# Ordering every engine by hand in a fused GNN and mixture-of-experts attention kernel, with a one-copy way out of PSUM for o

## The chip, the cores and the metric

The kernel runs on one core of a Trainium2 chip. The metric is the device time of one launch in microseconds; of several runs the median is given. Engines: TensorE (PE, its weight loads PEld), VectorE (DVE), ScalarE (ACT), GpSimd (POOL) and SyncE (SP). SP and POOL issue the DMAs that are spoken of here.

## The reference

A graph layer over 1250 nodes is followed by a block of attention with mixtures of experts and a feed-forward net. Only the second half of the attention is touched. With 16 heads of 64, 8 experts, 2 chosen, and rows of 1024:

```
q, k = rope(x Wq), rope(x Wk)                     # 16 heads of 1250 x 64
gv, go = gate(x, Wsel_v), gate(x, Wsel_o)         # sigmoid, top 2 of 8
v   = einsum('bsd,bhse,hedp->bhsp', x, gv, Wv)    # all 8 experts, gated sum
att = softmax(q k^T / sqrt(64))
o   = einsum('bhst,bhtp->bhsp', att, v)
y   = einsum('bhsp,bhse,hepd->bsd', o, go, Wo)    # added to the normalised input
```

Everything is float32. The kernel splits each factor of a product into a rounded part `hi` and the rest `lo`, and forms three matmuls, hi·hi, hi·lo, lo·hi (`dot`, lines 141 to 145). ACT rounds (`w_hi`, `att_hi`, `go_hi`), DVE subtracts (`w_lo`, `att_lo`, `go_lo`).

## The kernel before

Three Python generators issue the work, and the one that is not leading is stepped once per piece of the leading one.

- `values` leads first. Per head it splits four weight tiles of 128 x 1024 (`weights`, lines 123 to 134: load on SP into one of two `w_raw` buffers, `w_hi` on ACT, `w_lo` on DVE; five pairs of buffers are in rotation), then makes ten blocks of v. A block is 24 matmuls of 512 columns in four pieces of six. DVE multiplies a block by its gates (`ve`, line 808), and after every second block adds the experts in a tree (lines 814 to 819).
- `attention` runs under it, in chunks of 256 queries, five to a head and eighty in all, each of eight pieces. A chunk has two softmax blocks: PE makes `side`, DVE the maximum `most` (line 710), ACT the exp `p` (line 711). `turn` then moves the two blocks by 16 DMAs into `turned` (line 724), half issued by SP and half by POOL, DVE transposes within 32 x 32 blocks (line 787), and `split` makes `att_hi` and `att_lo` in five parts (lines 737, 738). `product` multiplies each part with v into the one PSUM tile `po` (line 751). v holds hi in columns 0 to 63 and lo in 64 to 127, so `po` has two halves of 64 rows, which belong together. Chunk n's softmax, chunk n-1's first two products and chunk n-2's last three lie in the same eight pieces.
- `outputs` leads after `values`, and the last pieces of `attention` run under it. Per pair of heads and half of the experts it splits four tiles of Wo, and in five steps of 250 nodes loads o (`oc`), 1/sum (`r`) and the gates (`gb`), multiplies them (lines 841, 850), splits the result (lines 853, 855), makes four groups of twelve matmuls, and adds each to `acc` (line 870). Then `feed_forward` follows.

The end of a product group is this; `po` has a single buffer, and the next group waits until both lines have read it:

```
nc.scalar.copy(o, po[HD:])                        # line 757, ACT
nc.vector.tensor_tensor(o, po[:HD], o, ALU.add)   # line 758, DVE
```

The order of PE is that of the program text in `values`, in `attention` and in the outputs that run with it (a manual schedule for PE alone). The order of the other engines there, and of all in the rest, is chosen by the framework's scheduler.

Of the kernel before, what the change touches and what calls it, by code (L numbers as in the profile page):

```python
# [22 lines left out]
N = 1250  # L23
# [49 lines left out]
def gnn_ffn_kernel(  # L73
# [31 lines left out]
    o_d = [dram.tile([P, N], F32, name=f"o_d{j}") for j in range(NP)]  # L105
# [11 lines left out]
    gate_v = base.tile([P, NT, P], F32, name="gate_v")  # L117
# [5 lines left out]
    def weights(block, lo_engine=None, raw=None):  # L123

        if raw is None:
            raw = raws[0].tile([P, D], F32, name="w_raw")
        nc.sync.dma_start(raw, block)
        pool = ring.pop(0)
        ring.append(pool)
        hi = pool.tile([P, D], F32R, name="w_hi")  # L130
        nc.scalar.copy(hi, raw)  # L131
        lo = pool.tile([P, D], F32R, name="w_lo")
        (lo_engine or nc.vector).tensor_tensor(lo, raw, hi.bitcast(F32), ALU.subtract)  # L133
        return hi, lo
# [54 lines left out]
    with ExitStack() as gctx:  # L189
# [314 lines left out]
        z_ctx = ctx.enter_context(ExitStack())  # L504
        zpool = z_ctx.enter_context(tc.tile_pool(name="zpool", bufs=1, side="right"))
# [16 lines left out]
    zpool2 = z_ctx.enter_context(tc.tile_pool(name="zpool2", bufs=1, side="right"))  # L522
# [156 lines left out]
    def attention(pool):  # L679
# [11 lines left out]
        def load(n):  # L691

            h, c = chunks[n]
            if c == 0:
                nc.gpsimd.dma_start(keys[:, :N], kq_d[h][:, 0, :].bitcast(F32R))
            q_of[n] = pool.tile([P, 2, QW], F32R, name="q", bufs=2)
            c0 = min(QW * c, N - QW)
            nc.gpsimd.dma_start(q_of[n], kq_d[h][:, 1:, c0 : c0 + QW].bitcast(F32R))

        def softmax(n, i):  # L700
# [12 lines left out]
            if i == 1:  # L713
                del q_of[n]

        def turn(n):
# [4 lines left out]
            for b in range(NA):  # L721
                for a in range(NA):
                    queue = nc.gpsimd if (a + b) % 2 else nc.sync
# [9 lines left out]
        def split(n, k):  # L733

            x = turned[n].rearrange("p t (A k) -> p (t A) k", A=NA)[:, :, 2 * NB * k : 2 * NB * (k + 1)]
            hi, lo = (pool.tile([P, 2 * NA, 2 * NB], F32R, name=name, bufs=3) for name in ("att_hi", "att_lo"))
            nc.scalar.copy(hi, x)  # L737
            nc.vector.tensor_tensor(lo, x, hi.bitcast(F32), ALU.subtract)  # L738
            parts_of[n, k] = hi, lo

        def product(n, k):
            h, c = chunks[n]
            if k == 0:
                sum_of[n] = psums[-1].tile([P, QW], F32, name="po", bufs=1)
            po = sum_of[n]
            parts = parts_of.pop((n, k))
            for b in range(2):
                t = 2 * k + b
                rows = min(P, N - P * t)
                for part in parts:  # L750
                    nc.tensor.matmul(po, lhsT=v_of[h][:rows, t, :], rhs=part[:rows, :, NB * b : NB * (b + 1)],  # L751
                                     start=(t == 0 and part is parts[0]), stop=(t == NT - 1 and part is parts[1]))
            if t < NT - 1:
                return
            del sum_of[n], turned[n]
            o = pool.tile([HD, QW], F32, name="o", bufs=1)
            nc.scalar.copy(o, po[HD:])
            nc.vector.tensor_tensor(o, po[:HD], o, ALU.add)  # L758
            j, h2 = divmod(h, 2)
            c0, new = min(QW * c, N - QW), QW * c  # L760
            to = o_d[j][HD * h2 : HD * (h2 + 1), c0 : c0 + QW]
            if (2 * n) % 3 < 2:
                nc.sync.dma_start(to[:, new - c0 :], o[:, new - c0 :])
            else:

                nc.sync.dma_start(to[:, new - c0 : P], o[:, P + new - c0 :])
                nc.sync.dma_start(to[:, P:], o[:, :P])

        load(0)
        for n in range(len(chunks) + 2):  # L770
            now, last, before = (0 <= m < len(chunks) for m in (n, n - 1, n - 2))
            for piece in range(8):
                if now and piece in (0, 3):
                    softmax(n, piece // 3)
                if piece == 3 and n + 1 < len(chunks):
                    load(n + 1)
                if now and piece == 3:
                    turn(n)
                if now and piece == 5 and chunks[n][1] == NC - 1:
                    sums(chunks[n][0])  # L780
                if before and piece in (1, 2, 4):
                    product(n - 2, min(piece + 1, 4))
                if last and piece > 5:
                    product(n - 1, piece - 6)
                if last and piece == 2:
                    for i in range(2):
                        nc.vector.transpose(turned[n - 1][:, i], turned[n - 1][:, i])  # L787
                if last and piece > 2:
                    split(n - 1, piece - 3)
                yield  # L790


    def values(att_pool, pool):
        for h in range(H):
            w = [weights(wv[h, k]) for k in range(4)]
            v_of[h] = att_pool.tile([P, NT, P], F32R, name="v2", bufs=2)
            for t in range(NT):
                n = min(P, N - P * t)
                p = bank([n, 512])
                for d in range(ND):  # L800
                    dot(p, z_of(t, d), [part[:, 512 * (d % 2) : 512 * (d % 2 + 1)] for part in w[d // 2]],
                        d == 0, d == ND - 1)
                    if d % 2 and d < ND - 1:
                        yield
                gate = gate_v[:n, t, NX * h : NX * (h + 1)]
                if t % 2 == 0:
                    ve = pool.tile([P, 2, NX, HD], F32, name="ve", bufs=1)
                nc.vector.tensor_tensor(ve[:n, t % 2], p.rearrange("p (e k) -> p e k", e=NX),
                                        gate[:, :, None].to_broadcast([n, NX, HD]), ALU.mult)
                if t % 2:  # L810
                    for n, k in ((P, slice(0, 2)),) if n == P else ((P, slice(0, 1)), (n, slice(1, 2))):
                        x = ve[:n, k]
                        for half in (4, 2):
                            nc.vector.tensor_tensor(x[:, :, :half], x[:, :, :half], x[:, :, half : 2 * half], ALU.add)
                        v = pool.tile([P, 2, HD], F32, name="v")[:n, k]
                        nc.vector.tensor_tensor(v, x[:, :, 0], x[:, :, 1], ALU.add)
                        v2 = v_of[h][:n, t - 1 + k.start : t - 1 + k.stop, :]
                        nc.vector.tensor_copy(v2[:, :, :HD], v)
                        nc.vector.tensor_tensor(v2[:, :, HD:], v, v2[:, :, :HD].bitcast(F32), ALU.subtract)
                yield  # L820
# [4 lines left out]
    def outputs(acc_pool, pool):  # L825
        last = QW * (NC - 1)
        for j in range(NP):
            for half_e in range(2):
                first = j == 0 and half_e == 0
                w = [weights(wo[j, 4 * half_e + i]) for i in range(4)]  # L830
                for c in range(NQ):
                    o = pool.tile([P, QB], F32, name="oc", bufs=1)
                    nc.sync.dma_start(o, o_d[j][:, QB * c : QB * (c + 1)])
                    r = pool.tile([P, QB], F32, name="r", bufs=1)
                    for h2 in range(2):
                        for a, b in ((QB * c, min(QB * (c + 1), last)), (max(QB * c, last), QB * (c + 1))):
                            if b > a:
                                at_ = a + (NC * QW - N if a >= last else 0)
                                nc.sync.dma_start(r[HD * h2 : HD * (h2 + 1), a - QB * c : b - QB * c],
                                                  r_d[j][h2 : h2 + 1, at_ : at_ + b - a].to_broadcast([HD, b - a]))  # L840
                    nc.vector.tensor_tensor(o, o, r, ALU.mult)
# [189 lines left out]
```

## Time and profile before

| what | value |
|---|---|
| median of three runs | 3069.24 us (3068.29 to 3071.58) |
| profiled execution | 3064.65 us, its span 3062.8 us |
| mean granted TensorE clock | 0.975 |
| busy share of PE, DVE, ACT, POOL | 94%, 69%, 33%, 16% |
| values and attention, from the first `turned` to the last product | 637.8 to 2056 us |
| first output matmul | 1953.3 us |
| output matmuls end | 2935.9 us |

A line of a group reads: source line, engine, operation, out<-in with the tiles' names, shape, count | busy time in us, mean ns of one | idle time of the engine just before, and what ended most of it. Matmuls are pipelined and overlap, so that the distance from start to start tells their rate. A wait for several things is put down to the one that came last.

### The profile page before, as it was taken

Reading aid. Unit: us, or ns where it says so; the run is one execution under the profiler, and the core shown is the slowest. Engines: PE = TensorE matmul, PEld = TensorE weight load, DVE = VectorE, ACT = ScalarE, POOL = GpSimd, SP = SyncE. Lnnn points to the kernel's source line nnn. Section 1 sums busy time; section 2 is a strip of 40 time slices with the busy share of each in tenths; the row PEclk is TensorE's granted clock in tenths of the full one; section 3 lists DMA queues with packets and bytes.
Section 4 is the critical chain, followed back from the end, with each engine's and each line's share of the span. In section 5 each row is a group of like instructions: output and inputs, shape, how many; then the busy total and the mean of one; then the engine's idle time right before and its main releaser. Section 6 shows DMA issues by size and latency. Waiting matters only on the chain. (4 is left out here: it accounts for less than half of the span.)

```text
span 3062.8 us, 40809 instructions
## 1 busy us (share of the span) xinstructions
PE 2883.5 (94%) x14018; PEld 2367.9 (77%) x14018; DVE 2099.1 (69%) x3731; ACT 1015.6 (33%) x1706; POOL 504.7 (16%) x838
## 2 busy tenths in 40 slices
PE   6989899999999999999998999789999999999998
PEld 5777799877777888777777887567777777777787
DVE  7975588567777787777776777665555555555685
ACT  5762223234444344434443344321111112111222
POOL 2000011123233232322322232110000000000023
PEclk9999899999999999999999999889999999999999
DMA  3115455635555555555554556755334334334312
GB/s 114 54 42 184 142 160 160 199 94 141 126 128 123 128 130 136 133 125 126 140 126 108 128 129 158 167 131 146 97 98 116 97 91 117 97 98 119 91 41 94
DMA packets 241546, 370.10 MB, mean 121 GB/s; under 512 B 61929, under 2 KB 191273, under 8 KB 241170
## 3 DMA queue, kind: packets, MB, share of 16 engines
q1 hardware_dynamic: 191854, 263.25, 31.7%
q0 software_dynamic: 47616, 93.93, 13.4%
q10 hardware_dynamic: 1860, 10.24, 1.1%
q8 instruction: 111, 1.82, 0.2%
q14 instruction: 105, 0.86, 0.1%
HBM read 210.49 MB, written 57.04 MB: 87 GB/s over the span
## 5 line engine op out<-in xcount | busy, mean ns | idle before, releaser
L145 PE MATMUL mm<-w_hi,go_lo 128*125 128x512 f32 x1280 | 507.7, 401 | 21.9 <-DVE go_lo L855 21.5
L143 PE MATMUL mm<-w_hi,go_hi 128*125 128x512 f32 x1280 | 510.6, 399 | 12.1 <-ACT go_hi L853 11.3
L143 PE MATMUL mm<-w_hi,zT 128*128 128x512 f32 (+1 forms) x1280 | 512.2, 400 | 0.0
L144 PE MATMUL mm<-w_lo,go_hi 128*125 128x512 f32 x1280 | 512.1, 400 | 0.0
L145 PE MATMUL mm<-w_hi,zT 128*128 128x512 f32 (+1 forms) x1280 | 511.7, 400 | 0.0
L144 PE MATMUL mm<-w_lo,zT 128*128 128x512 f32 (+1 forms) x1280 | 511.1, 399 | 0.0
L724 POOL DMA_DIRECT2D turned<-p x640 | 341.3, 542 | 355.3 <-ACT p L711 250.1
L737 ACT CAST att_hi<-turned 128x512 fp32r<-128x512 f32 x400 | 237.2, 619 | 440.3 <-PE po L751 187.7
L145 PEld LDWEIGHTS mm<-w_hi,go_lo 128*125 128x125 f32 x1280 | 240.9, 188 | 94.6 <-DVE go_lo L855 34.3
L710 DVE TENSOR_REDUCE most<-side 128x1 f32<-128x1250 f32 x160 | 232.6, 1454 | 116.2 <-PE side L707 104.7
L711 ACT ACTIVATE p<-side,most 128x1250 f32<-128x1250 f32 x160 | 209.0, 1306 | 309.9 <-DVE most L710 308.5
L738 DVE TENSOR_TENSOR att_lo<-turned,att_hi 128x512 fp32r<-128x512 f32 x400 | 262.8, 686 | 55.8 <-ACT att_hi L737 54.9
L143 PEld LDWEIGHTS mm<-w_hi,go_hi 128*125 128x125 f32 x1280 | 240.7, 188 | 72.8 <-ACT go_hi L853 12.2
L787 DVE STREAM_TRANSPOSE turned<-turned 128x1280 f32<-128x1280 f32 x160 | 232.3, 1490 | 92.6 <-DMA o_d<-o 63.3
L751 PE MATMUL po<-att_hi,v 128*128 128x256 f32 (+1 forms) x800 | 219.4, 295 | 78.6 <-DVE o L758 75.2
L145 PEld LDWEIGHTS mm<-w_hi,zT 128*128 128x128 f32 (+1 forms) x1280 | 241.3, 189 | 61.8
L853 ACT CAST go_hi<-gb 128x500 fp32r<-128x500 f32 x160 | 98.2, 614 | 571.6 <-PE mm L144 540.4
L144 PEld LDWEIGHTS mm<-w_lo,go_hi 128*125 128x125 f32 x1280 | 240.1, 188 | 58.8
L850 DVE TENSOR_TENSOR gb<-gb,oc 128x500 f32<-128x500 f32 x160 | 101.6, 676 | 251.2 <-DMA gb<-g_d 250.6
L144 PEld LDWEIGHTS mm<-w_lo,zT 128*128 128x128 f32 (+1 forms) x1280 | 241.9, 189 | 36.1
L143 PEld LDWEIGHTS mm<-w_hi,zT 128*128 128x128 f32 (+1 forms) x1280 | 241.7, 189 | 36.1
L133 DVE TENSOR_TENSOR w_lo<-w_raw,w_hi 128x1024 fp32r<-128x1024 f32 x154 | 187.6, 1218 | 103.1 <-ACT w_hi L131 102.9
(207 smaller groups left out, 4642.2 us busy)
## 6 DMA issues: line engine op xcount, KB each, us to landing
turned<-p SPq DMA_DIRECT2D x640, 80.0 KB
turned<-p POOLq DMA_DIRECT2D x640, 80.0 KB, 3.6
gb<-g_d SPq DMA_DIRECT2D x160, 250.0 KB
w_raw<-in_wv SPq DMA_DIRECT2D x64, 512.0 KB
w_raw<-in_wo SPq DMA_DIRECT2D x64, 512.0 KB
q<-kq_d POOLq DMA_DIRECT2D x80, 256.0 KB, 3.2
kq_d<-qk_hi SPq DMA_DIRECT2D x64, 156.2 KB
kq_d<-qk_lo SPq DMA_DIRECT2D x64, 156.2 KB
```

The lines of the kernel that those rows point to most:

```text
L133: (lo_engine or nc.vector).tensor_tensor(lo, raw, hi.bitcast(F32), ALU.subtract)
L143: nc.tensor.matmul(p, lhsT=lhs[0], rhs=rhs[0], start=start, stop=False)
L144: nc.tensor.matmul(p, lhsT=lhs[0], rhs=rhs[1], start=False, stop=False)
L145: nc.tensor.matmul(p, lhsT=lhs[1], rhs=rhs[0], start=False, stop=stop)
L710: nc.vector.tensor_reduce(most, side[:, :N], AX.X, ALU.max, negate=True)
L711: nc.scalar.activation(p[:, (2 * n + i) % 3, :N], side[:, :N], AF.Exp, bias=most, accum_out=inverse[h][:, 2 * c + i : 2 * c + i + 1])
L724: queue.dma_start(t[NB * a : NB * (a + 1), :, KA * b : KA * (b + 1)], both[NB * b : NB * (b + 1), :, KA * a : KA * (a + 1)])
L737: nc.scalar.copy(hi, x)
L738: nc.vector.tensor_tensor(lo, x, hi.bitcast(F32), ALU.subtract)
L751: nc.tensor.matmul(po, lhsT=v_of[h][:rows, t, :], rhs=part[:rows, :, NB * b : NB * (b + 1)], start=(t == 0 and part is parts[0]), stop=(t ...
L787: nc.vector.transpose(turned[n - 1][:, i], turned[n - 1][:, i])
L850: nc.vector.tensor_tensor(gb[:, :, mine], gb[:, :, mine], o[:, None, mine].to_broadcast([P, 4, KT]), ALU.mult)
```

## The change

- All five engines take the order of the program text in `attention`, `values` and `outputs`, and in the outputs after them up to the step where the feed-forward begins. The text was rewritten for that: `split` (ACT) and `rest` (DVE) are separate calls, and so are loading, rounding and the remainder of a weight; each is placed at a piece. The next head's four weights are spread over the pieces of the head before: in the lists of `values` `load` is the DMA, `first_part` makes `w_hi`, `second_part` makes `w_lo`, and the first number is the piece of the head (40 to a head).
- `o` leaves PSUM in one ACT copy of 128 rows and 256 columns; both halves are written to DRAM (by POOL, SP before), and `outputs` loads them as two planes and adds them there.
- The outputs' first weights, loads and parts are made under the last 16 pieces of `values`. For that the last head makes its blocks of v in the order 4 to 9, 0 to 3, and `acc` takes memory of the inputs that are done with. In each step the loads, the gating and the parts of the step after are made, and one weight of the next block.
- From then on `turn` issues all its 16 DMAs on POOL.
- The products and their order on PE stay as they are, apart from the order within the last head.

The diff, cut to its core:

```diff
-    o_d = [dram.tile([P, N], F32, name=f"o_d{j}") for j in range(NP)]
+    o_d = [dram.tile([2, P, N], F32, name=f"o_d{j}") for j in range(NP)]
...
-                    queue = nc.gpsimd if (a + b) % 2 else nc.sync
+                    queue = nc.gpsimd if (a + b) % 2 or main else nc.sync
...
         def split(n, k):
+            k = order(n, k)
...
             nc.scalar.copy(hi, x)
+            parts_of[n, k] = hi, lo, x
+
+        def rest(n, k):
+            hi, lo, x = parts_of[n, order(n, k)]
             nc.vector.tensor_tensor(lo, x, hi.bitcast(F32), ALU.subtract)
+
+        def order(n, k):
+            return (k + (NZ // 2 if chunks[n][0] == H - 1 else 0)) % (NT // 2)
...
-            o = pool.tile([HD, QW], F32, name="o", bufs=1)
-            nc.scalar.copy(o, po[HD:])
-            nc.vector.tensor_tensor(o, po[:HD], o, ALU.add)
+            o = pool.tile([P, QW], F32, name="o", bufs=1)
+            nc.scalar.copy(o, po)
...
-                nc.sync.dma_start(to[:, new - c0 :], o[:, new - c0 :])
+                nc.gpsimd.dma_start(to[:, new - c0 :], o[:, new - c0 :])
...
         for n in range(len(chunks) + 2):
             now, last, before = (0 <= m < len(chunks) for m in (n, n - 1, n - 2))
+            if now:
+                softmax(n, 0)
+            if before:
+                rest(n - 2, 4)
+            if n + 1 < len(chunks):
+                load_queries(n + 1)
+            yield
+            if before:
+                product(n - 2, 2)
+            if last:
+                turn_blocks(n - 1)
+            yield
+            if before:
+                product(n - 2, 3)
+            if last:
+                split(n - 1, 0)
+                split(n - 1, 1)
+            yield
+            if now:
+                softmax(n, 1)
+                if n + 1 < len(chunks) and chunks[n + 1][1] == 0:
+                    load_keys(chunks[n + 1][0])
+            if last:
+                rest(n - 1, 0)
+                rest(n - 1, 1)
+            yield
+            if before:
+                product(n - 2, 4)
+            if now:
+                turn(n)
+                if chunks[n][1] == NC - 1:
+                    sums(chunks[n][0])
+            if last:
+                split(n - 1, 2)
+            yield
+            if last:
+                rest(n - 1, 2)
+            yield
+            if last:
+                product(n - 1, 0)
+                split(n - 1, 3)
+            yield
+            if last:
+                product(n - 1, 1)
+                split(n - 1, 4)
+                rest(n - 1, 3)
+            yield
...
+    def values(att_pool, pool, now):
...
+                for at_, k in ((22, 0), (36, 1), (37, 2), (39, 3)):
+                    later(piece + at_, first_part, k)
+                for at_, k in ((23, 0), (37, 1), (38, 2), (40, 3)):
+                    later(piece + at_, second_part, k)
+                for at_, k in ((16, 0), (22, 1), (28, 2), (37, 3)):
+                    later(piece + at_, load, h + 1, k)
...
+            ts = range(NT) if h < H - 1 else [*range(NZ, NT), *range(NZ)]
...
     def outputs(acc_pool, pool):
...
+        def gated(gb, o, r):
+            nc.vector.tensor_tensor(o[:, 0], o[:, 0], o[:, 1], ALU.add)
+            nc.vector.tensor_tensor(o[:, 0], o[:, 0], r, ALU.mult)
+            nc.vector.tensor_tensor(gb, gb, o[:, 0:1].to_broadcast([P, 4, QB]), ALU.mult)
+            return gb
...
+        for m, (k, c) in enumerate(steps):
+            raw = loaded(blocks[k + 1][c]) if c < 4 and k + 1 < len(order) else None
+            following = steps[m + 1] if m + 1 < len(steps) else None
+            if following:
+                found = load(*order[following[0]], following[1])
+            for i in range(2):
+                t = 2 * c + i
+                if k == 0 and t + 1 < NT:
+                    acc_load(t + 1)
+                for half in range(2):
...
+                    nc.vector.tensor_tensor(acc[t][:, cols], acc[t][:, cols], p, ALU.add)
+                    if following and half:
+                        parts[i] = parts_of(found, i)
+                    elif following and i == 0:
+                        found = gated(*found)
+                    elif raw is not None:
+                        after.append(rounded(raw))
+                    yield
...
-            tc.manual_schedule(engines={mybir.EngineType.PE}):
+        w = [weights(wv[0, k]) for k in range(4)]
+        with tc.manual_schedule(engines=all_engines):
+            heads = attention(apool)
+            with tc.tile_pool(name="vpool", bufs=2) as vpool:
+                for k, _ in enumerate(values(apool, vpool, w)):
+                    if k >= per_head - lead:
+                        next(heads)
+                    if k == H * per_head - 4 * NZ - 1:
+                        z2_ctx.close()
...
+                        main.append(outputs(acc_tile, gop))
+                    elif main:
+                        next(main[0])
+            made = sum(1 for _ in zip(heads, main[0]))
...
+    with tc.manual_schedule(engines=all_engines):
+        for _ in range(4 * (NT * (2 * NP - 1) + 4) - made):
+            next(main)
+    next(tail)
```

## The prediction

> **What bounds the kernel now.** I read the page first: TensorE is busy nearly everywhere, so the end is set by the sum of its matmuls and the holes between them.
>
> ```profile
> PE 2883.5 (94%) x14018; PEld 2367.9 (77%) x14018; DVE 2099.1 (69%) x3731; ACT 1015.6 (33%) x1706; POOL 504.7 (16%) x838
> PEclk9999899999999999999999999889999999999999
> ```
>
> Then the waits of PE over the whole span, longest first (total us, times, longest): what the change could remove.
>
> ```profile
> PE po L751 <- DVE o L758: 75.2, 36, 7.8
> PE mm L145 <- DVE go_lo L855: 21.5, 22, 2.1
> ...
> PE mm L143 <- ACT go_hi L853: 11.3, 2, 10.7
> ```
>
> Then the stretches: heads under the values (653 to 1870), the passage into the outputs (to 2060), outputs alone (to 2863). The first numbers are length and PE busy, "PEclk" follows the engines.
>
> ```profile
> 653.00:1870.00 1217.00, 1158.31 (x5677) 957.35 (x5678) 945.84 (x1353) 494.35 (x771) 362.32 (x653) 0.98 0.54 129
> 1870.00:2060.00 190.00, 152.09 (x700) 123.34 (x699) 127.09 (x185) 64.12 (x102) 38.30 (x70) 0.89 0.63 146
> 2060.00:2863.00 803.00, 784.21 (x3321) 616.56 (x3320) 431.63 (x677) 137.61 (x192) 4.77 (x2) 0.99 0.41 108
> ```
>
> PE idles 58.7, 37.9 and 18.8 us there; the rest of the span the change does not touch. The timeline of POOL shows one head as five chunks: each chunk's eight `turned` issues start when its second exp ends.
>
> ```profile
> 1313.92 3.73 POOL L724 DMA_DIRECT2D turned<-p  x7 [3.56 <-ACT p L711]
> ...
> 1332.23 4.26 POOL L724 DMA_DIRECT2D turned<-p  x8 [6.00 <-DMA w_raw<-in_wv]
> ...
> 1352.01 4.25 POOL L724 DMA_DIRECT2D turned<-p  x8 [3.57 <-ACT p L711]
> ...
> 1367.93 4.26 POOL L724 DMA_DIRECT2D turned<-p  x8 [3.57 <-ACT p L711]
> ...
> 1384.63 4.28 POOL L724 DMA_DIRECT2D turned<-p  x8 [3.82 <-ACT p L711]
> ...
> 1400.24 3.73 POOL L724 DMA_DIRECT2D turned<-p  x7 [3.56 <-ACT p L711]
> ```
>
> The chunks take 18.3, 19.8, 15.9, 16.7, 15.6 us. Its matmuls alone: 48 value matmuls at 0.231 us start to start (1018.41, 1018.64, 1018.87 in the timeline) 11.1; two softmax blocks of four such and two of half size 2.3; 20 products at 0.118 2.4: 15.8. So quiet chunks already run at the floor of PE, 15.85 in most rows of all heads, and the loss lies at the two chunks where a head's four weights change. From chunk 0 (638.0) to chunk 73 (1886.8) the mean is 17.1: 73 x 1.26 = 92 us lost.
>
> The groups give DVE's load:
>
> ```profile
> L738 DVE TENSOR_TENSOR att_lo<-turned,att_hi 128x512 fp32r<-128x512 f32 x400 | 262.8, 686 | 55.8 <-ACT att_hi L737 54.9
> L787 DVE STREAM_TRANSPOSE turned<-turned 128x1280 f32<-128x1280 f32 x160 | 232.3, 1490 | 92.6 <-DMA o_d<-o 63.3
> L710 DVE TENSOR_REDUCE most<-side 128x1 f32<-128x1250 f32 x160 | 232.6, 1454 | 116.2 <-PE side L707 104.7
> L133 DVE TENSOR_TENSOR w_lo<-w_raw,w_hi 128x1024 fp32r<-128x1024 f32 x154 | 187.6, 1218 | 103.1 <-ACT w_hi L131 102.9
> ```
>
> Per chunk: 5 att_lo 3.43, 2 transposes 2.98, 2 maxima 2.91, 2 gated products 1.37, the tree 1.90, the add of o 0.41: 13.0, and 1.22 for each w_lo. DVE has slack in a quiet chunk and none in one with three w_lo; there `o`'s add sits behind them and PE, whose single `po` bank it frees, waits 5 to 8 us.
>
> **The change, part by part.** *o in one copy.* 80 adds of 0.408 leave DVE, and PE's release passes to one ACT copy (0.369 for 64 rows; for 128 rows I take the same, since 64- and 128-partition casts of 512 cost 0.617 and 0.619). The add returns in the outputs, 80 x 0.455 by the `oc` row, on a DVE that is half idle there (431.6 of 803): nothing. If that cover were gone it would cost 36. Writes of o double to 128 KB each: nothing, DMA share 0.54.
>
> *Order by hand, values stage.* I place each queue by the new order from time 0 of a chunk. PE: first softmax ends 2.54, second 8.79, po's last product 10.64, the next group wants po at 13.4. DVE: first maximum 2.8 to 4.3, att_lo to 5.0, gate 5.6, transposes 5.6 to 8.5, second maximum 9.1 to 10.5, two att_lo to 11.8, gate and tree 12.3 to 14.9, att_lo to 16.2: idle until 18.6. ACT: second exp to 11.9, o's copy 12.4, before 13.4. POOL now issues o's one or two writes (0.54 each) after that copy and ahead of its eight `turned`, which end 5.4 to 5.9 after the exp; SP's eight end at 6.5. Both land by about 8.5 to 9.7, where 8.5 is what the quiet chunks show. The quiet chunk stays at the floor.
>
> Chunk with the weights: ACT makes w_hi 1 before the second exp (0.2 late) and w_hi 2 ahead of o's copy, which ends 13.7: PE waits 0.3. SP's load of weight 3 waits for w_lo 1 (13.05) and stands ahead of this chunk's SP `turned`, which start 1.5 late. DVE: w_lo 1 at 11.8, w_lo 2 to 14.55, gate and long tree to 17.95, att_lo 18.6, w_lo 3 to 19.8, but PE wants w_lo 3 at 18.9: 1.0. The next transposes end 0.2 after the second softmax wants its maximum. So 1.3 a boundary, 15 boundaries: 20 kept. Bounds: 0, and the 7.1 a head loses now (86.3 less 5 x 15.85); I take the worked value. Behind the waiting SP load only `turned` is queued, for which the transposes wait.
>
> The clock is a second part of the 92: 0.98 over 1217 us is 24 us of lost clock. I keep 13 (between 0 and 24). I also keep 8 for a late landing whose cause the profile does not tell:
>
> ```profile
> 1656.63 2.90 DVE L787 STREAM_TRANSPOSE turned<-turned 128x1280 f32<-128x1280 f32 x2 [10.12 <-DMA turned<-p]
> ```
>
> Kept 41, gained 51.
>
> The Trainium skill, "TensorE: Matmul & The Clock Gate", Part 1, says that the clock halves only after an idle window of about 3.4 us. By that rule none of my 0.3 and 1.0 us waits would trip it, and the 13 would go as well (2962).
>
> *Passage.* From chunk 73's exp to the last product PE needs 3.85 + 6 x 15.85 + 13.4 + 8.3 = 121; it takes 170 (1886.8 to 2056.3), 49 lost: 11 for the first go_hi, whose loads and weights start too late, much of the rest for o. With the prelude 16 pieces earlier, its four w_lo, gating and parts (8.4 of DVE) lie in two chunks that have no next head's weights. But all 16 `turned` now go through POOL: o's copy and writes 1.4, 16 x 0.533 = 8.5, landing 3.1 after the last issue (3.6 less its 0.5): 13.3 after the exp instead of 8.5. The round transposes, maximum, exp, `turned` then takes 13.3 + 2.9 + 1.4 + 1.3 + 1.35 of output work queued between on DVE = 20.3, against 15.8 of PE work. PE waits, by the same placing, 3.2, 4.6, 4.6, 4.6 and 5.5: 22; with half clock after each, 6 more: 28 kept, 20 gained. Bounds: 16 kept (a landing as now) to 45 (landing 5.8, its 95th percentile, and a DVE that is late).
>
> The Trainium skill, "SBUF — State Buffer", section "SBUF: two separate sides", speaks against putting more DMAs on POOL: DVE in a 2-port mode locks out the descriptor writing of POOL's DMAs. Here POOL's 640 `turned` issues lie between 0.539 and 0.561 us whatever DVE does, so the trace shows no lockout. By the page each of the 16 could wait for a DVE instruction, and the passage would gain nothing (2995).
>
> *Outputs alone.* Loads, gating and parts stand a step (11.1 us of PE) ahead; SP needs some 5 us of issue a step, DVE 7.2. The 17.5 of go_lo and 0.9 of acc go, with half of the 8 us of clock: 23. Bounds 15 and 27: the work is the same, only earlier.
>
> *Sum.* 51 + 20 + 23 = 94. The profiled execution took 3064.65 us, 4.6 under the median of the runs: 3064.65 - 94 + 4.6 = 2975.
>
> **Rivals.** *A, the boundary stays dear.* With three w_lo DVE's chunk holds 16.3 us against 15.8 of PE; if in-order queues waste a few more, PE waits for w_lo 3 or the transposes instead of o, and the passage gains nothing. For: DVE is full there. Against: two quiet chunks recover it. Left are quiet-chunk waits (14) and outputs (23): 3032.
>
> *B, slower: the round of the transposition becomes the bound of every chunk.* Place: exp, `turned`, transposes, second maximum. It takes the landing plus 5.6, so it decides from a landing 10.2 us after the exp, and it eats all gains at 12.1, where chunk 0 to 73 lose (92 + 43) / 73 = 1.85 each. For: POOL's `turned` now queue behind o's copy and writes, and boundary chunks showed 11 to 13. Against: quiet ones show 8.5 to 9.5, and SP loses its writes of o. At 13 a chunk takes 18.6: 73 x 2.75 = 201 for 92, less 43: 3135.
>
> *C, nearly all holes close.* Boundaries, clock and passage and outputs all at the bounds that keep least: 84 + 33 + 27 = 144 gained, 2925.
>
> *D, nothing moves*: the waits pass from o to another DVE product in equal size, 3069.
>
> **How the numbers follow.** Forecast (2955 to 3000) 0.50, A 0.22, C 0.15, B 0.10, D 0.03. The range reaches from the upper half of C to past A: 2940 to 3050. Within 0.2% (some 6 us) is what a measurement of this kernel can tell from no change. Faster is forecast, A and C: 0.87; slower 0.11, same 0.02.
>
> **What would show it.** Right: no wait of PE for o above 10 us in all; chunks of 15.8 to 16 except one or two a head at 17; chunks 75 to 79 some 20 us apart, with DVE idle before its transposes for `turned`; after the passage, waits for go_lo gone and clock 1.0. Wrong: transposes that wait for `turned` in quiet chunks (B); PE waiting for w_lo 3 by several us a head (A); chunks 75 to 79 at 16, which would put my price of 16 POOL issues too high.

## The result and the profile after

The kernel after takes 3068.86 us in the median of 12 runs (3062.26 to 3081.66), the kernel before 3069.88 us in 12 runs beside it: ratio 0.9996, 95% interval 0.9982 to 1.001. The forecast was 2975. A second comparison gave 0.9996 again (0.9974 to 1.0018). The profiled execution of after took 3081.66 us (span 3079.9), 13 us above its median; before's took 3064.65.

Page of after, busy times and the granted clock:

```profile
PE 2874.7 (93%) x14018; PEld 2371.4 (77%) x14018; DVE 2130.1 (69%) x3651; ACT 993.9 (32%) x1706; POOL 591.5 (19%) x985
PEclk9999899999999999999999999789999999999999
```

Waits of PE in after, over the whole span (total us, times, longest). The change took DVE's add away from `po`, and yet PE waits longer for `po` than before (111 + 15 against 75):

```profile
PE po L771 <- ACT o L778: 111.4, 24, 12.9
PE po L771 <- DVE att_lo L753: 14.6, 1, 14.6
```

The three stretches in after, with bounds moved to where the stages now end (length, then PE, PEld, DVE, ACT and POOL busy, PEclk, DMA share, GB/s):

```profile
653.00:1900.00 1247.00, 1173.89 (x5764) 972.03 (x5763) 939.43 (x1304) 482.20 (x781) 423.61 (x759) 0.97 0.58 130
1900.00:2085.00 185.00, 120.82 (x549) 98.75 (x549) 104.78 (x142) 52.16 (x85) 60.31 (x111) 0.83 0.72 147
2085.00:2880.00 795.00, 793.91 (x3415) 631.60 (x3414) 491.01 (x697) 141.20 (x200) 7.16 (x4) 1.00 0.46 123
```

PE idles 73.1, 64.2 and 1.1 us there: the outputs alone are now full and at clock 1.00, as forecast; the two stages before them got worse. The group of the transposes says what is late: DVE's idle time before them went from 92.6 to 183.3 us, and what ended the largest part of it is `turned` instead of `o_d`.

```profile
L791 DVE STREAM_TRANSPOSE turned<-turned 128x1280 f32<-128x1280 f32 x160 | 232.3, 1490 | 183.3 <-DMA turned<-p 76.3
```

A ledger, cut at instructions that both kernels have (end of a chunk's second exp, end of an add into `acc`; profiled executions). The last column is an experiment told below (its second run), in which r_d is written in rows; changes in us:

| stretch | before | after | forecast | after less before | with rows, less before |
|---|---|---|---|---|---|
| second exp of chunk 0 to that of chunk 73 | 1248.8 | 1259.8 | -51 | +11.0 | -50.4 |
| to the first add of the outputs' second block | 176.1 | 203.2 | -20 | +27.1 | +10.0 |
| to the first add of their last block (14 blocks) | 814.2 | 784.1 | -23 | -30.1 | -30.2 |
| to the end | 186.2 | 194.5 | 0 | +8.3 | +6.4 |

With the 0.7 us ahead of chunk 0 this is the 17.1 by which the two spans differ. So the outputs gave more than the forecast, the end lost 8 (in part two waits of PE, 3.0 us for the last add into `acc` and 2.7 for `sT`), and the forecast broke in the first two rows.

**Where the values stage lost.** I call the time from the end of a chunk's second exp to the start of its transposes its turn time. In after it is 9.4 to 10.2 us in most quiet chunks, and their period 15.0 to 15.9: the floor. (The chunks 5h + 3, h being the head, are a little later: 10.6 and 16.3 in the mean.) But seven chunks, 9, 19, 24, 29, 39, 54 and 69, have 16 to 22 us and a period of 22 to 28. All are last chunks of a head (5h + 4), where `sums` writes the head's 1/sum to r_d. Chunk 9 in the timeline of after, POOL, SP and DVE (start, length, engine, line, operation, tiles, count, idle time before and its end):

```profile
788.21 0.56 POOL L786 DMA_DIRECT2D o_d<-o  x1 [2.81 <-ACT o L778]
788.76 0.55 POOL L787 DMA_DIRECT2D o_d<-o  x1
789.62 4.29 POOL L734 DMA_DIRECT2D turned<-p  x8 [0.31 <-DMA turned<-p]
...
787.68 5.08 SPq L734 DMA_DIRECT2D turned<-p  x8
792.87 0.53 SPq L741 DMA_DIRECT2D r_d<-some  x1
793.45 2.36 SPq L127 DMA_DIRECT2D w_raw<-in_wv  x2
...
804.37 2.91 DVE L791 STREAM_TRANSPOSE turned<-turned 128x1280 f32<-128x1280 f32 x2 [7.55 <-DMA turned<-p]
```

All 16 `turned` are issued by 793.9, r_d goes out between them, and the transposes start 10.5 us after the last issue. The view of the DMA engines for 786 to 806 in 40 slices of half a microsecond (busy tenths, then GB/s) shows the hole: from 796.5 on the engines count as busy for a tenth to nine tenths of the time, but move only 16 to 51 GB/s together, for 8 us.

```profile
DMA  9499506896797998979987942729526998131579
GB/s 150 100 440 380 210 23 141 200 231 180 169 220 187 284 295 282 261 152 119 121 123 21 20 31 23 49 16 31 51 18 39 25 47 43 27 29 27 129 258 348
```

r_d's write is one DMA of 1280 pieces of 4 bytes. In before the same write is there, but the chunk is not late:

```profile
790.25 4.28 POOL L724 DMA_DIRECT2D turned<-p  x8 [2.99 <-ACT p L711]
...
789.98 6.36 SPq L724 DMA_DIRECT2D turned<-p  x8
796.44 0.53 SPq L766 DMA_DIRECT2D o_d<-o  x1
...
797.72 0.53 SPq L731 DMA_DIRECT2D r_d<-some  x1
...
798.95 2.91 DVE L787 STREAM_TRANSPOSE turned<-turned 128x1280 f32<-128x1280 f32 x2 [1.35 <-DMA o_d<-o]
```

There POOL's half ended 3 us before r_d and SP's half had o's writes behind it; the engines moved at most 7 GB/s from 798.5 to 803, so `turned` had landed when the pieces ran, and no weights were being loaded. One chunk of before, 59, in which POOL's half ended 0.4 us after r_d's issue, was late too (17.7 us): the "late landing whose cause the profile does not tell" of the prediction.

### The profile page after: what moved, and what is told of

Read it like the earlier page. It is cut to its first block, busy times and chain, and to the rows that moved or that the text cites. A ratio compares the mean times of both kernels' runs of the same rounds, so it can differ in the third digit from the quotient of the medians.

```text
span 3079.9 us, 40353 instructions
## 1 busy us (share of the span) xinstructions
PE 2874.7 (93%) x14018; PEld 2371.4 (77%) x14018; DVE 2130.1 (69%) x3651; ACT 993.9 (32%) x1706; POOL 591.5 (19%) x985
## 5 line engine op out<-in xcount | busy, mean ns | idle before, releaser
L155 PE MATMUL mm<-w_lo,zT 128*128 128x512 f32 (+1 forms) x1280 | 511.9, 400 | 10.2 <-DVE w_lo L144 10.2
L734 POOL DMA_DIRECT2D turned<-p x680 | 364.0, 542 | 120.8 <-ACT p L723 44.4
L791 DVE STREAM_TRANSPOSE turned<-turned 128x1280 f32<-128x1280 f32 x160 | 232.3, 1490 | 183.3 <-DMA turned<-p 76.3
L999 DVE TENSOR_TENSOR zT<-zT,mm 125x512 f32<-125x512 f32 x256 | 175.4, 686 | 223.8 <-PE mm L156 219.8
L771 PEld LDWEIGHTS po<-att_hi,v 128*128 128x128 f32 (+1 forms) x800 | 157.0, 196 | 142.2 <-ACT o L778 124.2
```

Of the source, the lines that this page charges most:

```text
L155: nc.tensor.matmul(p, lhsT=lhs[0], rhs=rhs[1], start=False, stop=False)
L734: queue.dma_start(t[NB * a : NB * (a + 1), :, KA * b : KA * (b + 1)], both[NB * b : NB * (b + 1), :, KA * a : KA * (a + 1)])
L791: nc.vector.transpose(turned[n][:, i], turned[n][:, i])
L999: nc.vector.tensor_tensor(acc[t][:, cols], acc[t][:, cols], p, ALU.add)
```

## Experiments

Each run is read against before on its own chip. Before stood at 3070 to 3072 us in three groups of runs and at 3099 to 3105 in three others, so ratios are compared, or kernels of one group.

**1. r_d in rows, in after and in before.** The tile of sums is padded to 32 columns, turned, and leaves in 40 rows of 128 bytes:

```diff
-            nc.sync.dma_start(r_d[h // 2][h % 2].rearrange("(k r) -> r k", r=P), total)
+            nc.vector.transpose(total, total)
+            to = r_d[h // 2][h % 2].rearrange("(k a r) -> a k r", a=P // NB, r=NB)
+            for a in range(P // NB):
+                nc.sync.dma_start(to[a], total[NB * a : NB * a + 2 * NC, :])
```

> The kernel after, but the sums of a head go to r_d in rows of 128 bytes: the tile of 10 sums a partition is padded to 32, turned by a 32x32 transpose on VectorE, and written by four DMAs of ten rows, in place of one DMA of 1280 pieces of 4 bytes. Theory 1 (the pieces hold up what is issued beside or behind them: the POOL `turned` of the head's last chunk, then the weight loads and the `turned` of the next head's first chunk, the first Wo load in the passage, r and oc at its end): the seven chunks with 16 to 22 us from exp to transposes fall to 10 (7 x 6 = 42 us), the first chunks of the heads from 17-19 us to 16-17 (14 x 1.5 = 20), the passage loses 10 to 20 less; together 3069 - 75 = about 2995, at most 3015. Theory 2 (POOL's order, o's writes ahead of `turned`, and the order on ACT and SP at the head's start): the late chunks stay late whatever r_d is written in, under 15 us gained, 3055 to 3070.

> The kernel before with the same four DMAs of 128-byte rows for r_d. Theory 1 in its narrow form (in the kernel before the pieces fell into slack, because SP issued o's writes between its `turned` and r_d; only the change brought them onto the path): 0 to 20 us gained, 3050 to 3069. Theory 1 in its wide form (they cost the kernel before as much): 50 to 75 gained, 2995 to 3020. Theory 2: no change.

> The kernel after with r_d in 128-byte rows once more, so that the three kernels built on it are compared on one chip: about 3007 us again, 0.98 of before where before is 3070.

> The kernel before with r_d in 128-byte rows, on a chip of this group, to be read against a_rows_again (3001 where before is 3072). If only the pieces' cost depends on the chip: 3055 to 3062 again, 10 to 15 us less than before here, and the change without the pieces is worth 3058 - 3001 = 57 us. If it follows before's time: 3031.

After with rows: 3007.64 us, 0.969 of before (0.9671 to 0.9708), and 3001.18, 0.9769 (0.9743 to 0.9794), in the second group. Ahead of the passage no chunk has more than 14.5 us, most chunks 5h + 4 have 10 and chunks 5h fell from 11 to 9.7. Chunk 9 in the second of the two runs:

```profile
790.86 1.94 SPq L745 DMA_DIRECT2D r_d<-some  x4
...
794.72 2.91 DVE L795 STREAM_TRANSPOSE turned<-turned 128x1280 f32<-128x1280 f32 x2 [0.84 <-DMA r_d<-some]
```

r_d is issued at the same place, 5.3 us behind the exp, and the transposes start at 9.2 instead of 16.8. So the pieces are shown to cost after 68 us (3069.0 to 3001.2, before at 3071 in both groups). Before with rows: 3061.99, 0.986 (0.9836 to 0.9884), and 3065.47, 0.988: 40 us gained in groups where before stood at 3103 and 3105. It was not run beside a before at 3070. The only profile of before is from a group at 3070, and against it the profiles of before with rows are 7 to 8 us shorter in the values stage (1241.4 and 1240.6 us) and 10 to 12 in the passage, but 16 to 18 longer in the outputs, whose order the scheduler chose anew: the spans are equal (3062.6 and 3062.8). So where the 40 us went is not shown. As the kernels with rows differ by 7 us or less between groups and before by 35, most of that spread seems to be the pieces' own. In one group the change is worth 3061.99 to 3007.64, 54 us, once the pieces are gone from both. In those groups the wide form of my theory came nearer than the narrow one: before paid as well. Against a before at 3070, by times of different groups, it would be 4 to 10 us, as the narrow form had it.

**2. r_d later.** Same pieces, but the DMA's text stands behind the next chunk's transposes.

> The kernel after, with the 1280 pieces of 4 bytes as they are, but r_d's DMA is issued one chunk later, behind the transposes of the head's last chunk, when its `turned` have landed. Theory 1 (it is the overlap of the pieces with other transfers): the chunks 5h + 4 fall from 16-22 us to 10 (7 x 6 = 42 us gained); the pieces, 8 to 10 us long, then reach into the `turned` of chunk 5h of the next head, 5 us behind the transposes, which go from 11 to 13-16 us (15 x 2 to 4 = 30 to 60 us given back): between 30 faster and 20 slower than after. Rival (the chunks 5h + 4 are late for another reason, such as the order on POOL): they stay at 16 us.

3030.40 us, 0.9886 (0.9842 to 0.9929), 39 less than after in that group. SP does not wait for DVE, so r_d did not go out after the landing, as I had meant, but only 0.6 to 2.7 us later and behind one load of weights. That was enough to bring the chunks 9, 24, 39 and 54 from 15 to 17 us to 12 to 13 and the chunks 5h from 11.2 to 10.1. For these the rival (another cause) is out; chunk 29 still has 18.8.

**3. What of the change exposed the pieces.** Three trials: o's writes on POOL in the kernel before; in after, o's write issued behind `turned` on POOL; in after, the load of weight 1 moved from behind r_d. In after the loads of weights 1 and 2 both stand there. The second edit is shortened here.

```diff
# before: o's writes
-                nc.sync.dma_start(to[:, new - c0 :], o[:, new - c0 :])
+                nc.gpsimd.dma_start(to[:, new - c0 :], o[:, new - c0 :])
# after: order on POOL
-                product(n - 2, 4)                     # with o's write
-                turn(n)
+                out = product(n - 2, 4); turn(n); o_out(n - 2, *out)
# after: place of a load
-                for at_, k in ((16, 0), (22, 1), (28, 2), (37, 3)):
+                for at_, k in ((16, 0), (18, 1), (28, 2), (37, 3)):
```

> The kernel before, one part of the change alone: the writes of o to o_d go from SP to POOL, so that on SP r_d's write comes right behind the `turned` of the chunk. Theory 1: the chunks with r_d (5h + 4) whose POOL half of `turned` is issued later than SP's go from 10 us between exp and transposes to 16, as in after; 5 to 8 of 16 chunks, 25 to 50 us slower than before. Theory 2: `turned` on POOL stands behind o's write (about 0.5 us a chunk), which quiet chunks hide: 0 to 10 us slower, spread over all chunks alike.

> The kernel after with r_d's 4-byte pieces as they are, but on POOL the chunk's eight `turned` are issued ahead of o's write, so that they start 0.3 us behind exp and not 1.6 to 2.1, and end some 1.5 us sooner, over 1 us before r_d goes out on SP. Theory 1 (the pieces overtake a `turned` issued less than about 1 us before them): the late chunks 9, 24, 39, 54 (16-17 us) fall to 10, chunk 29 too; 5 x 6 = 30 us gained against after, 3040; the first chunks of the heads stay at 11 to 12. Rival (the pieces hold up whatever is in flight, with or without a lead): the 16-us chunks stay, 3060 to 3070.

> The kernel after with r_d's 4-byte pieces and its place as they are; only the load of weight 1 goes out four pieces (half a chunk) earlier, so that none stands behind r_d on SP. Theory 5 (a lead of `turned` over r_d did not help by itself; the pieces cost where 0.5 MB of weights comes right behind them, as in after and not in the kernel before with o on POOL): the chunks 5h + 4 fall to 9-10 us but for two or three, the chunks 5h from 11 to 10; 3020 to 3040 where after is 3069 (0.985 to 0.99 of before). Rival (the pieces hold the last `turned` by themselves): the chunks 9, 24, 39, 54 stay at 16, 5h + 0 gains 1 us: 3050 to 3070.

Before with o on POOL: 3074.90, 1.0017 (0.9998 to 1.0037), two late chunks (18.0 and 16.2) instead of one: not the 25 to 50 us expected. `turned` ahead of o's write: 3073.22, 0.9904 (0.9881 to 0.9926) beside a before of 3105; with a lead of some 3 us over r_d (but in chunk 29, where POOL is late) all chunks 5h + 4 lie at 12 to 17 us, so the lead alone does not save them. In before with o on POOL r_d has the same place (2.3 to 3.0 us behind POOL's last `turned`, 0.1 us behind SP's), but there no load of weights follows within 20 us, q's load stands ahead of `turned` on POOL and not behind, and only two chunks are late. Load moved: 3072.83, 0.9914 (0.9893 to 0.9935) beside a before of 3099; chunks 9, 24, 39, 54 and 69 have 17 to 19 us. But the edit did not do what was meant by it: the load of weight 2 moved up and now stands right behind r_d. Chunk 9 in that run:

```profile
788.24 5.10 SPq L734 DMA_DIRECT2D turned<-p  x8
793.45 0.53 SPq L741 DMA_DIRECT2D r_d<-some  x1
794.07 1.73 SPq L127 DMA_DIRECT2D w_raw<-in_wv  x1
```

So 0.5 MB behind the pieces are no better than 1 MB, but r_d with no load behind it was not tried in after, and theory 5 is not settled; the comparison of the first two kernels speaks for it, or for the place of q's load. Loads are not needed for a late chunk: before has one, and two with o on POOL, without any. What the three profiles with r_d straight behind SP's `turned` and o's write ahead of POOL's (after twice, load moved) have in common: where r_d leaves 0.4 us or more before POOL's last `turned` (those five, 69 in two of the three, and 29), the chunk is late by 4 to 12 us; where it leaves with that one or behind it, mostly not, with exceptions (19, 59, 64, and 69 once). Overtaking does harm, and not overtaking is no safe pass. Which transfer the pieces hold up, and where in the chip, stays open.

**4. The passage: who issues, or how much is loaded.** Half of `turned` back on SP (`or main` taken out), without and with rows; and rows without the loads of z into `acc`.

> The kernel after, but half of the 16 `turned` of each chunk stay on SP in the passage too (the words `or main` taken out). Theory 3 (the 16 on POOL are what makes the passage's chunks 28 to 30 us): landing falls from 20-24 us after exp to about 14, 4 chunks x 7 = 28 us gained, about 3040. Rival (the outputs' loads fill the DMA engines, whoever issues `turned`; and SP's half now waits behind those loads): landing stays above 20 us, 0 to 10 us gained or lost.

> Both edits at once. If the two causes are apart: the sum of the two gains, about 2970 by theories 1 and 3; if r_d's pieces were what crowded the passage, the gain is that of the rows alone.

> The kernel after with r_d in 128-byte rows, and without the loads of z_d into acc (ten of 512 KB in the passage): the first products are copied into acc instead of added, so the residual is left out of the result. Theory 4 (in the passage the DMA engines are the bound: turned 1.3 MB, q and o 0.4, the outputs' loads 2.4 a chunk, 4.1 MB in 25-27 us = 155 GB/s): with 1.0 MB less a chunk the landing falls from 20-24 us after exp to about 15-17, the periods from 27-30 to 21-24, 5 x 5 = 25 us gained against the kernel with the rows alone, about 0.8%. Rival (POOL's lane waits, 13 to 16 us to issue 16 `turned`, set the landing): they stay, under 8 us gained.

Half on SP: 3091.06, 0.9956 (0.9937 to 0.9976); turn times of chunks 75 to 78 are 17.9, 20.5, 21.2, 20.1 (after: 20.4, 23.6, 23.3, 12.9). With rows 3002.63 against 3007.64: 5 us. POOL's 16 issues are not what fills the passage. Without the loads of z: 2989.18, 0.9746 (0.9705 to 0.9787); turn times 14.5 and 17.4 in chunks 76 and 77 instead of 24.3 and 22.2, and the passage 18 us shorter, as the theory of the full DMA engines had it. Chunk 76's exp ends at 1898.3 in both kernels; the engines from 1898 to 1938 in slices of 1 us, rows alone:

```profile
DMA  6499999999999999999999994000000000978999
GB/s 144 127 279 295 254 256 300 333 163 172 249 246 214 222 253 246 217 173 216 175 238 218 180 111 95 16 0 0 0 0 0 0 0 16 168 94 312 298 207 205
```

and without z:

```profile
DMA  5788699999789991000000005899999998996390
GB/s 155 120 283 319 143 310 191 230 225 241 154 234 271 214 227 28 0 0 0 0 0 0 0 0 160 127 303 320 209 215 199 224 194 174 276 237 218 62 224 0
```

The engines are full at some 220 GB/s, for 25 us with the loads and 15 without.

**5. The head's edge.** Load of weight 3 one piece later, behind SP's `turned`; w_hi 2 behind o's copy; w_lo 2, w_hi 3, w_lo 3 later.

```diff
-                for at_, k in ((22, 0), (36, 1), (37, 2), (39, 3)):     # first_part
+                for at_, k in ((22, 0), (36, 1), (38, 2), (41, 3)):
-                for at_, k in ((16, 0), (22, 1), (28, 2), (37, 3)):     # load
+                for at_, k in ((16, 0), (22, 1), (28, 2), (38, 3)):
```

> The rows, and the head's edge put in another order: the load of weight 3 comes one piece later, behind the `turned` of chunk 5h + 1 on SP, w_hi 2 one piece later, behind o's copy on ACT, and w_lo 2, w_hi 3 and w_lo 3 one or two pieces later. Theory 2 (at the edge the order costs, not the transfers): from exp to transposes 12.3 us falls to 10 to 10.5 in the chunks 5h + 1, their period from 17.9 to 16.2, 15 x 1.7 = 25 us gained against the rows alone, 0.8%. Rival (the load of weight 3 and the `turned` share the DMA engines whoever comes first; and w_hi 3, which now waits for a later load, stands ahead of the next exp on ACT): under 8 us gained, or up to 30 lost with waits of ACT for w_raw.

3114.72, 1.0138 (1.0107 to 1.0169), 113 us slower than the rows alone: chunks 5h + 1 take 25.2 us instead of 17.9, 15 x 7.3 = 110. The load, issued at 1018.6 in chunk 21, landed as w_hi 3 shows, and ACT's next exp stood behind that:

```profile
1025.39 1.04 ACT L138 CAST w_hi<-w_raw 128x1024 fp32r<-128x1024 f32 x1 [9.33 <-DMA w_raw<-in_wv]
```

The change's order, which lets `turned` wait 0.9 to 1.7 us for the load, is the better one.

**6. Putting parts together.** z loaded later (two places), then with `turned` first, and with the edge on ACT's queue.

```diff
# z late: steps 6 to 15, one tile a step     # or: pairs, in steps c = 4 of blocks 1 to 5
-            move(acc[t], z_d[t])
+                zx = raws[0].tile([P, D], F32, name="w_raw")[:KT]
+                move(zx, z_d[tz])
...
+                        nc.vector.tensor_tensor(acc[tz], acc[tz], zx, ALU.add)
```

> The rows, and z_d loaded later: the first products are copied into acc, and each of the ten tiles of z is loaded into a free w_raw buffer and added on VectorE one a step in steps 6 to 15, in the stage of the outputs alone. Theory 4: the passage gains what it gained without these loads (18 us against the rows alone), and the outputs hide the loads (0.5 MB in 16 us beside a DMA share of 0.4) and the ten adds of 1.3 us on a VectorE that is 60 to 65% busy: 15 to 18 gained. Rival: the loads hold up the outputs' own in the later stage and the gain is given back, 0 to 8.

> Rows, edge and late z together, and half of `turned` on SP in the passage (`or main` taken out). If the parts add up: 25 + 17 + 5 us less than the rows alone, about 2960 where before is 3070; if the edge gains nothing, 2985.

> The rows; `turned` ahead of o's write on POOL; half of `turned` on SP in the passage; and z loaded in the last block of the outputs, where no weights are loaded (two tiles a step into w_raw's buffers, added before the products). Against the rows alone (0.977 of before): 17 to 20 us in the passage, now not given back in the outputs' blocks 1 and 2, which went from 55.9 to 63.8 and 59.0 us with the late z before; 0.3 to 0.5 us a chunk, 20 to 30 us, from POOL's earlier `turned` if the quiet chunks' period follows the landing, nothing if it stands at PE's 15.8. 2955 to 2985 where before is 3072.

> As the kernel before in this list, and the head's edge: weight 3 is loaded by ACT's queue behind o's copy, so that SP's `turned` no longer stands behind it, w_hi 2 comes behind o's copy, w_hi 3 and w_lo 3 one piece later. Chunk 5h + 1: SP's `turned` start 0.1 us behind exp instead of 1.7, L from 12.3 to 10.5-11, 15 x 1.3 = 20 us gained against it; if the load lands behind w_hi 3's place on ACT (the edge experiment's 6.7 us from issue), ACT and the next exp wait 1 to 3 us, 15 to 45 us lost.

> The rows, and z loaded in pairs in the steps c = 4 of the outputs' blocks 1 to 5, where no weight is loaded, into w_raw's two buffers, and added in the same step. Passage as without the loads of z (15 to 18 us less than the rows alone), blocks 1 to 5 at 55.9 us as before: 0.972 of before, 2985 where before is 3070; if the pair holds up the next block's weights, 3 to 5 us a block are given back, 0.977.

z in steps 6 to 15: 2996.83, 0.9755 (0.9727 to 0.9783); the passage gained 15, blocks 1 and 2 gave 9 back (63.8 and 59.0 us instead of 57.4 and 55.9). The edge undid all in the second kernel (3123.67, 1.017). The third: 3033.52, 0.9779 (0.9734 to 0.9824), worse than rows alone in the values (16.71 a chunk against 16.45): SP's eight issues take some 7 us where POOL's eight start at the same time and mostly 5.1 to 5.9 where POOL starts behind o's write, and quiet chunks turn in 10.8 to 11.2 us in the mean instead of 10.1 to 10.8. The longer issue alone does not explain it: in before SP's eight take 6.0 to 7.4 us and quiet chunks turn in 9.0 to 9.2 in the mean. z in the last block made that 12 us longer. The fourth, 3057.62, 0.985, adds waits of PE for w_lo (34.8 us instead of 12.7). The last, rows and z in pairs: 2990.37, 0.9651 (0.9634 to 0.9667) beside a before of 3099, the fastest that forms the whole result, 11 to 17 us under the rows alone in other groups, with blocks 1 to 5 at 55.9 to 57.7. Its stretches:

```profile
653.00:1900.00 1247.00, 1204.29 (x6004) 996.72 (x6002) 984.01 (x1392) 503.40 (x814) 446.42 (x797) 1.00 0.55 138
1900.00:2085.00 185.00, 161.87 (x704) 130.01 (x705) 125.01 (x168) 48.41 (x78) 46.47 (x76) 0.92 0.61 149
```

PE idles 42.7 and 23.1 us where after had 73.1 and 64.2.

## Why the prediction was wrong

- **Values stage, "both land by about 8.5 to 9.7 ... the quiet chunk stays at the floor": right for most quiet chunks** (9.4 to 10.2, floor held), and the step that failed is that every chunk of a head was costed as one of two kinds, quiet or with weights. The chunk with r_d is a third. I listed POOL's new place behind o's writes and the loss of o's writes on SP as harmless, and did not follow the next thing in SP's queue, r_d, which is in no term of the sum. With rows the stage is 50.4 us shorter than in before, where the forecast had 51, and a chunk takes 16.42 us in the mean, where it had 15.85 + 41/73 = 16.41. That the two agree so well is luck: I kept 20 for boundaries, 13 for the clock and 8 for a late landing, and the run keeps 30 in the chunks 5h + 1, 8 in the chunks 5h + 3 (16.4 us each) and 3 in the rest. So the term left out was the pieces, 68 of the 94 us by which the forecast missed. The rest, by the profiles, is the passage (30 short with the rows) and the end (6), less the 7 that the outputs gave above the forecast. PE's waits for o, of which at most 10 us were to be left, are 111.
- **Boundary chunks, 1.3 us each: too low.** They take 17.9 us with rows, 2 us over the floor, 30 in all instead of 20. The PE wait for w_lo 3 is the 1.0 forecast (13 us in 16 waits), but the turn time is 12.3, not under 10.2: SP's `turned` start 0.9 to 1.7 us late (1.5 forecast), and they are in flight together with the load of weight 3, which I had counted at its issue only. That this load is what slows them is argued, not shown.
- **Clock, 13 us kept: too much once the long waits are gone.** From chunk 0 to 73 the stretches at half clock (3.4 us and multiples of it in the clock records) cost before 27 us and after 32, but the kernels with rows 3 to 5. There the longest wait of PE in the values is 2.6 and 3.8 us, in after 11.1. The rule that the prediction weighed, of the Trainium skill's page "TensorE: Matmul & The Clock Gate", Part 1 (an idle window of about 3.4 us), came near in the sum, as by it all 13 were to go. But as a threshold it does not hold here: waits of 2.35 us (before, to 1162.9), 1.99 (after, to 739.7) and 1.80 (first run with rows, to 1321.9) were each followed by half clock (0.50 in after from 740.9 to 744.3), while one of 2.70 (after, to 913.3) was not.
- **Passage, landing 13.3 us after the exp: the term that was mis-sized.** Where SP loads nothing, in chunk 78, the turn time is 12.9: 16 issues take 8.5 us, as I said, but they start 2.7 us behind the exp and land 1.7 behind the last, where I had 1.4 and 3.1, so that the sum agrees by luck in part. In chunks 75 to 77 it is 20.4, 23.6 and 23.3, and the chunks are 28 to 30 us apart, not 20. Chunk 76 in after's timeline, its exp ends at 1968.2:

```profile
1970.54 3.74 POOL L734 DMA_DIRECT2D turned<-p  x7 [0.61 <-DMA r<-r_d]
1976.31 0.54 POOL L734 DMA_DIRECT2D turned<-p  x1 [2.02 <-DMA o_d<-o]
...
1983.17 0.54 POOL L734 DMA_DIRECT2D turned<-p  x1 [0.74 <-DMA turned<-p]
1991.83 2.90 DVE L791 STREAM_TRANSPOSE turned<-turned 128x1280 f32<-128x1280 f32 x2 [12.21 <-DMA q<-kq_d]
```

  The 16 issues took 13.2 us instead of 8.5, as POOL had to wait between them for earlier transfers, and the landing was 8 us after the last issue, not 3.1 (chunk 77 the same; chunk 75 spent its time in the issues, 13.9 us, which POOL began 3 us late). I had taken the latency from the values stage, at a DMA share of 0.54, into a stage in which each chunk also loads a step's weights, gates, o, r and z (2.4 MB beside `turned`'s 1.3). SP issues a step's loads when DVE is done with the gating that stands just ahead of the maximum for the exp, so they start together with `turned`. Without z's loads the turn times of chunks 76 and 77 fell by 10 and 5 us (experiment 4), which shows z's loads as a cause; half of `turned` on SP did little (5 us). POOL's issues of `turned` took 0.54 us in the mean in after too, so a lockout of POOL by DVE, which the prediction weighed, is not seen. Two more waits stand behind r_d: the first Wo load, issued right behind it, for which w_hi and with it an exp of chunk 75 waited 9.6 us on ACT, and the loads of r issued by SP in chunk 79, 10.3 us long, with DVE 16.6 us idle for `oc`.
- **Outputs alone, 23 gained: right in kind, too low**, 30, where my bound was 27.
- **o in one copy, 0.369 us: right** (0.36 in the timeline). That part alone was not run.
- **Rivals.** B named the place, the turn round, and its point of decision (10.2 us), but put it in all chunks and its cause in POOL's queue; it ruled in 7 chunks and in the passage, and the transfers were the cause. A's and B's "for" lines both looked at engines' queues; none of my four looked at the transfers.

The Trainium skill, "DMA: Bandwidth & Descriptors", section "Specifications", gives 512 bytes as the least transfer for full rate and says that below it the engine reads, modifies and writes. By that rule 128-byte rows are as bad as 4-byte pieces, only fewer. The run shows that fewer is enough: with 40 rows a head no chunk ahead of the passage has more than 14.5 us, with 1280 pieces seven have 16 to 22.

## What to carry to other kernels

Price a DMA by its pieces as well as its bytes, and follow what goes out beside it: a write of 5 KB in 4-byte pieces cost this kernel 68 us over 16 uses, and four DMAs of rows behind a 0.2 us transpose took that away. Take latencies from the stage in which the transfer will run: the sum of bytes that one round sets off, divided by the rate seen with the engines full (some 220 GB/s here), estimates the least time of that round. An order by hand removes the slack that hid such things; before fixing one, list for every queue what moves next to what.

## What the runs showed of the hardware

- The pieces of r_d pass the queues within some 2 us, and then the 16 DMA engines together moved 16 to 51 GB/s for 8 us (chunk 9 above); a load of q issued 1 us behind r_d landed after 14 us, where the median is 4.8. Where all else had landed and no load followed (chunk 9 of before), nothing was late.
- Eight `turned` on SP mostly took 5.1 to 5.9 us to issue when POOL's eight came 1.4 to 1.9 us later, and 6.3 to 7.2 when both started together; POOL's own eight took 4.3 in both cases.
- POOL is 3 us late in every 23rd chunk of after's text (6, 29, 52, 75 in both profiles of it), ahead of its `turned`; chunk 29, where r_d goes out at the same time, is the latest of the values stage (22 us). The cause stays open.
- The time of before varied by 35 us between groups of runs, that of the kernels with rows, each in two groups, by 7 or less.
